# A sparse graph layer: one place column instead of sixteen, and three of 41 gathers taken from DRAM by indirect DMAs

## The chip, the cores and the metric

The kernel runs on one core of a Trainium2 chip. The metric is device time in microseconds (us), the median of several executions; lower is better. The core has five engines that run side by side and are tied together by semaphores: TensorE (PE, with its weight loads as PEld), VectorE (DVE), ScalarE (ACT), GpSimd (POOL) and SyncE (SP). In this kernel SP issues nearly all DMAs, each in its order, and waits in front of one for what that DMA needs. POOL issues DMAs of its own on a second queue.

## The reference

32 independent graphs (batches) of N = 512 nodes, D = 128 features, and a weighted adjacency of which about one entry in 16 is not zero (and the diagonal). Layer 0 is a normalized graph convolution with a residual and a layernorm. Layer 1 forms a message for every ordered pair of nodes and sums the messages with the adjacency as weight:

```python
m_j = einsum('bnd,do->bno', x, W1[:D])
m_i = einsum('bnd,do->bno', x, W1[D:])
pre = m_j[:, None, :, :] + m_i[:, :, None, :] + b1      # one vector per pair (i, j)
msg = gelu(layernorm(pre, g1, be1))
agg = einsum('bijo,bij->bio', msg, adjacency)
upd = layernorm(concatenate([x, agg]) @ W2 + b2, g2, be2)
x   = layernorm(x + upd)
```

Dense, this would be 512 x 512 messages a batch. The kernel computes only those whose adjacency is not zero.

## The kernel before, in words

**The tiling.** The nodes of a batch are cut into C = 4 chunks of P = 128. A source node j sits on a partition; chunk q holds 128 sources. For each source and each target chunk c, the nonzero targets are kept as a list. The first SLOTS = 8 entries of a list are its slots t = 0 to 7. Slot 8 (`EXTRA`) is the ninth entry of the lists inside a chunk's own diagonal block. What is left over in the lists of one (q, c) block is packed into 256 shared places, which are slots 9 and 10. A *group* is one slot t of one source chunk q, for the four target chunks: 4 x 128 messages. There are 8 x 4 + 1 + 2 x 4 = 41 groups in a batch (`order`), numbered n = 0 to 40 here; group 18 is (t 4, q 2), group 22 is (5, 2) and group 26 is (6, 2).

**One group's work.** `pairs` (L720 to L725) makes `u`, a PSUM bank of 4 x 128 x 128: for each target chunk three bf16 products of a one-hot matrix `s` with the three bf16 parts `c3` of the target's vector c = m_i + b1 (L724, a gather by product), and a fourth product with the standard deviations (L725). In the shared slots a float32 product adds the source's vector (L720). `sums` (L734, DVE) adds the source's vector a and writes `u_sb`. `messages` (L763, ACT) applies gelu with the pair's own scale, four instructions per group. `weights` (L749, POOL) multiplies the transposed one-hots `mt` with the adjacency into `sw`. `aggregate` (L772, PE) sums `m` x `sw` into one PSUM bank `agg` for the whole batch.

**The pipeline over groups.** In round n of the main loop the program writes down `pairs` of group n, `aggregate` of n-3, `sums` and `weights` of n-1 and `messages` of n-2. `u` has 3 buffers, `u_sb` 3, `m` 3, `sw` 4, so an engine that falls back by about two groups stops PE. On ACT, POOL and DVE the order of instructions is the order in which the program writes them (`manual_schedule`). On PE and SP a list scheduler orders them.

**The side work.** The preparation of the next batch and of the later slots of this one is cut into steps by `yield` and spread over the rounds by the table `plan` (phase, steps, first and last round). `layer0`, `lists` (the eight largest of each list with their indices, L399 and L400, and `idx_d`, which is sent through DRAM), `parts` (`ac`, the vectors a and c; POOL adds a bias at L622; then `c3` by three ACT casts L627 with a POOL subtraction L626 between them), `factors`, `more` (16 further entries of each list, L455 to L458) and `shared` follow each other and overlap. `parts` of the next batch lies in rounds 22 to 30 of the present one, `shared` in rounds 8 to 27.

**`shared` in detail.** `a_t` holds for each block the transposed adjacency (128 columns) and 3 x 16 more: the place numbers of the 16 further entries, their node numbers and their variances; `WIDE` = 176. POOL fills the place columns with two operations on 128x256 (L502, L505). A float32 product with the one-hot `sj` sends the rows of `a_t` to their places (L537, 32 products of 128x176 per batch, each in two passes in the trace), ACT copies the banks to `sent` (L533). DVE then picks from each sent row the entry whose place equals the row's own place (L553, four operations, and L561, two reductions into `picked`). ACT and PE turn `picked` into `idx_ds` (L566, L574, L582), which goes through DRAM to `raw` and comes back as one-hot `s` of slots 8 to 10. POOL waits for `picked` at L578.

## Time and profile before

| | |
|---|---|
| median of 3 runs | 4012.79 us (4010.46 to 4013.59) |
| the profiled execution's own time | 4011.93 us |
| its span (first to last instruction on the core) | 4010.2 us |
| PE busy in the span | 3759.7 us, 94% |
| DVE, ACT, POOL busy | 81%, 69%, 56% |
| granted TensorE clock, mean | 0.985 |
| time of one batch in the steady part (from one `agg` start after a wait for ACT to the same one six batches later, 1079.73 to 1819.44 us) | 123.3 us |

A batch is a fixed succession of stretches that repeats 32 times, so the profile is best read on one batch (here the one from 2028 to 2152 us) and multiplied. A row of the groups gives line, engine, operation, output <- inputs, shape, count, then busy time, mean duration of one, and the idle time just before it with what ended it. Matmul durations overlap each other, so the price of a matmul is taken from the distance of starts in the timeline.

### The profile page before, as it was taken

What the parts mean: (1) busy time and instruction counts of PE and PEld (TensorE: products, weight loads), DVE (VectorE), ACT (ScalarE), POOL (GpSimd) and SP (SyncE); (2) the same over time, 40 slices, a digit from 0 to 9 for tenths busy, and PEclk for the clock granted to TensorE, in tenths of its full rate; (3) what the DMA queues carried; (4) which work ended last, traced back from release to release, by engine and by line L of the source; (5) the groups of instructions that cost most, each with busy time, mean ns of one, the idle gap of its engine ahead of it and who ended that gap; (6) DMA issues with size and microseconds to landing.
All of it is one profiled execution on the core that took longest, in us unless ns stands there. A gap on an engine that the chain in (4) does not pass through costs nothing. (4 is left out here: it accounts for less than half of the span.)

```text
span 4010.2 us, 108407 instructions
## 1 busy us (share of the span) xinstructions
PE 3759.7 (94%) x39744; PEld 3502.1 (87%) x39744; DVE 3262.1 (81%) x10645; ACT 2785.8 (69%) x8321; POOL 2226.4 (56%) x2526
## 2 busy tenths in 40 slices
PE   5999999999999999999999999999999999999997
PEld 5988889888899888998888988889988889888887
DVE  6888888888887888888888878888888888788882
ACT  4777677676676766777766777667777667776664
POOL 4555565555654555655556556566556565565654
PEclk7999999999999999999999999999999999999998
DMA  3444444444544544444444444444444444444442
GB/s 85 106 109 106 115 100 106 109 104 105 115 100 106 106 104 111 106 108 107 108 105 107 104 110 104 104 113 105 108 108 106 107 103 107 111 104 104 100 106 56
DMA packets 902107, 419.99 MB, mean 105 GB/s; under 512 B 724304, under 2 KB 882192, under 8 KB 901568
## 3 DMA queue, kind: packets, MB, share of 16 engines
q1 hardware_dynamic: 901344, 412.52, 44.3%
q8 instruction: 317, 5.19, 0.5%
q14 instruction: 222, 1.82, 0.1%
q0 software_dynamic: 224, 0.46, 0.1%
HBM read 227.15 MB, written 13.76 MB: 60 GB/s over the span
## 5 line engine op out<-in xcount | busy, mean ns | idle before, releaser
L749 POOL TENSOR_TENSOR sw<-mt,a_t 128x512 f32<-128x512 bf16 x1056 | 1216.5, 1164 | 918.4 <-PE agg L772 767.5
L772 PE MATMUL agg<-sw,m 128*128 128x128 f32 x10496 | 1494.0, 285 | 109.5 <-ACT m L763 64.3
L724 PE MATMUL u<-c,s 128*128 128x128 bf16 x15744 | 1411.5, 220 | 58.1 <-DVE u_sb L734 54.5
L763 ACT ACTIVATE m<-u_sb,r 128x128 f32<-128x128 f32 x4096 | 1293.3, 394 | 196.3 <-DVE counts L484 105.9
L772 PEld LDWEIGHTS agg<-sw,m 128*128 128x128 f32 x10496 | 1301.9, 193 | 131.9 <-POOL ve_l L199 67.7
L724 PEld LDWEIGHTS <-s 128*128 128x128 bf16 x15744 | 1191.9, 99 | 136.4 <-issue 64.4
L725 PE MATMUL u<-be,sd_rows 128*128 128x128 bf16 x5248 | 1148.6, 220 | 21.4 <-DMA sd_rows<-sd_ds 15.5
L734 DVE TENSOR_TENSOR u_sb<-u,ac 128x512 f32<-128x512 f32 x1056 | 713.4, 676 | 199.1 <-PE u L725 176.8
L725 PEld LDWEIGHTS <-sd_rows 128*128 128x128 bf16 x5248 | 514.8, 98 | 31.5 <-issue 20.8
L763 ACT ACTIVATE m<-u,r_s 128x128 f32<-128x128 f32 x1024 | 288.9, 363 | 251.9 <-PE agg L772 247.9
L687 DVE TENSOR_SCALAR s<-raw,node_p 128x2052 bf16<-128x2052 bf16 (+1 forms) x352 | 421.5, 1197 | 20.4 <-DMA raw<-idx_ds 11.8
L720 PE MATMUL u<-ac,sj 128*128 128x128 f32 x2048 | 437.2, 295 | 0.0
L749 POOL TENSOR_TENSOR sw<-mt,sent 128x512 f32<-128x512 bf16 x256 | 296.5, 1163 | 226.6 <-PE agg L772 188.7
L533 ACT COPY sent<-pl 128x352 f32<-128x352 f32 x512 | 229.1, 447 | 258.3 <-PE pl L537 221.4
L537 PEld LDWEIGHTS pl<-a_t,sj 128*128 128x128 f32 x2048 | 316.1, 190 | 60.1 <-issue 37.1
L457 DVE MAX8 a_t<-key 128x8 f32<-128x128 f32 x1024 | 301.2, 295 | 34.5
L537 PE MATMUL pl<-a_t,sj 128*128 128x176 f32 x2048 | 327.4, 313 | 0.6 <-POOL a_t L505 0.6
L522 DVE TENSOR_SCALAR sj<-pj,node_p 128x512 f32<-128x512 f32 x256 | 187.6, 745 | 156.4 <-PE pj L526 156.4
L720 PEld LDWEIGHTS u<-ac,sj 128*128 128x128 f32 x2048 | 309.8, 191 | 0.4
L458 DVE FIND_INDEX8 idx_m<-a_t,key 128x8 uint32<-128x128 f32 x1024 | 291.4, 285 | 0.0
L361 DVE SCALAR_TENSOR_TENSOR key<-pv,a_sum,c_sum 128x512 f32<-128x512 f32 x128 | 95.6, 748 | 108.3 <-PE pv L365 108.3
L400 DVE FIND_INDEX8 idx<-top,key 128x8 uint32<-128x128 f32 x512 | 145.7, 285 | 0.0
(178 smaller groups left out, 4766.5 us busy)
## 6 DMA issues: line engine op xcount, KB each, us to landing
raw<-idx_d SPq DMA_DIRECT2D x256, 513.0 KB
raw<-idx_ds SPq DMA_DIRECT2D x64, 513.0 KB
a_nat<-in_adj_dram SPq DMA_DIRECT2D x32, 1024.0 KB
sd_rows<-sd_d SPq DMA_DIRECT2D x768, 12.0 KB
xs<-in_x_dram SPq DMA_DIRECT2D x32, 256.0 KB
out_dram<-o_sb SPq DMA_DIRECT2D x32, 256.0 KB
mt<-s SPq DMA_TRANSPOSE x352
raw<-idx_ds SPq DMA_DIRECT2D x32, 129.0 KB
```

The lines of the kernel that those rows point to most:

```text
L457: nc.vector.max(found, k)
L458: nc.vector.max_index(idx[:, n, h : h + 8], found, k)
L533: nc.scalar.copy(sent[:, n - 1], pt[:, : SHARED * WIDE].rearrange("p (k w) -> p k w", w=WIDE))
L537: nc.tensor.matmul(pt[:, k * WIDE : (k + 1) * WIDE], sj[:, n, k * P : (k + 1) * P], at[:, n, :], start=True, stop=True,)
L687: nc.vector.tensor_scalar(s.rearrange("p (k e) -> p k e", k=3), raw, node_p, None, ALU.is_equal)
L720: nc.tensor.matmul(pu[:, c, :], place, state[b]["ac"][:, q, 0, :], start=first, stop=False)
L724: nc.tensor.matmul(pu[:, c, :], here, c3[:, k, c, :], start=(first and k == 0), stop=False)
L725: nc.tensor.matmul(pu[:, c, :], dev[:, q, c, :], be9, start=False, stop=(c == C - 1))
L734: nc.vector.tensor_tensor(u, pu, a if t == EXTRA else bcast(a[:, q, :], C), ALU.add)
L749: nc.gpsimd.tensor_tensor(sw, mt[:, 0] if t == EXTRA else mt[:, :, q, :], a, ALU.mult)
L763: nc.scalar.activation(m[:, c, :], u[:, c, :], AF.Gelu, scale=r[:, k : k + 1])
L772: nc.tensor.matmul(st["agg"][:, c, :], m[:, c, :], sw[:, c, :], start=(begin and c == 0), stop=(end and c == C - 1),)
```

## The change

Two edits stand in one diff. First, the sixteen place columns in `a_t` become one column, which holds the place that entry 0 of the list has or would have (`first` + `sharing`). `WIDE` becomes 161. POOL writes it with one operation on 128x16. At the receiving side `rank` = own place - first place tells which of the sixteen entries is meant, and DVE compares `nth` (now counted from 0) with it: two operations on 16 elements, two comparisons of 256, two multiplications of 512 and the two reductions as before. `shared` has 46 steps instead of 45.

Second, for the groups 18, 22 and 26 the three gather products per target chunk (12 per group) are left out. Instead `parts` writes c (512 x 128 float32, 256 KB) to DRAM (`c_d`) on the SP queue, between POOL's bias addition and its first subtraction, which overwrites the same tile; `parts` has 8 steps instead of 7. `lists` computes row numbers `row_no` with three small DVE operations. In the rounds 5, 4, 3 and 2 before such a group, POOL issues one indirect DMA each, which fetches 128 rows of 512 bytes by `row_no` into `c_i`. DVE adds the source's vector to `c_i` in the group's own round, and `sums` adds `c_i` instead of a broadcast vector.

```diff
-WIDE = 128 + 3 * MORE
+WIDE = 128 + 2 * MORE + 1
@@ constants
-        nth, pattern=[[0, C * C], [1, MORE]], base=1, channel_multiplier=0, allow_small_or_imprecise_dtypes=True
-    nc.gpsimd.tensor_scalar(nth[:, own, :], nth[:, own, :], 1.0, None, ALU.subtract)
+        nth, pattern=[[0, C * C], [1, MORE]], base=0, channel_multiplier=0, allow_small_or_imprecise_dtypes=True
+    chunk_0 = const.tile([P, C], I32, name="chunk_0")
+    nc.gpsimd.iota(chunk_0, pattern=[[P, C]], base=0, channel_multiplier=0)
@@ lists, after the last max_index
+        row_no = small.tile([P, len(by_rows), C], I32, tag="row_no", name=f"row_no_{b}", bufs=1)
+        for k, (t, q) in enumerate(by_rows):
+            nc.vector.tensor_tensor(row_no[:, k, :], idx[:, q * C : (q + 1) * C, t], chunk_0, ALU.add)
+        st["row_no"] = row_no
@@ shared
-        place, node_i, var = (at[:, :, P + k * MORE : P + (k + 1) * MORE] for k in range(3))
+        node_i, var = (at[:, :, P + k * MORE : P + (k + 1) * MORE] for k in range(2))
...
-        nc.gpsimd.tensor_tensor(
-            place, nth, first.unsqueeze(2).to_broadcast([P, C * C, MORE]), ALU.add
-        )
-        nc.gpsimd.tensor_tensor(place, place, over, ALU.mult)
+        nc.gpsimd.tensor_tensor(at[:, :, WIDE - 1], first, sharing[:, :, 0], ALU.add)
...
+        rank = small.tile([P, SHARED, C * C], F32, tag="rank", name=f"rank_{b}", bufs=1)
+        for k in range(SHARED):
+            nc.vector.tensor_scalar(
+                rank[:, k, :], sent[:, :, k, WIDE - 1], place_k[:, k : k + 1], -1.0, ALU.subtract, ALU.mult
+            )
+        for k in range(SHARED):
+            nc.vector.tensor_tensor(
+                chosen[:, 1, k], nth, rank[:, k, :].unsqueeze(2).to_broadcast([P, C * C, MORE]), ALU.is_equal
+            )
+        yield
         for h in range(2):
-            for k in range(SHARED):
-                nc.vector.scalar_tensor_tensor(
-                    chosen[:, h, k],
-                    sent[:, :, k, P : P + MORE],
-                    place_k[:, k : k + 1],
-                    sent[:, :, k, P + (1 + h) * MORE : P + (2 + h) * MORE],
-                    ALU.is_equal,
-                    ALU.mult,
-                )
+            nc.vector.tensor_tensor(
+                chosen[:, h],
+                chosen[:, 1],
+                sent[:, :, :, P + h * MORE : P + (h + 1) * MORE].rearrange("p n k l -> p k n l"),
+                ALU.mult,
+            )
             nc.vector.tensor_reduce(picked[:, h, :], chosen[:, h].rearrange("p k n l -> p (k n) l"), AX.X, ALU.add)
@@ parts
         nc.gpsimd.tensor_tensor(rest, rest, bcast(b1g, C), ALU.add)
+        yield
+        c_d = dram.tile([N, D], F32, tag="c_d", name=f"c_d_{b}")
+        nc.sync.dma_start(c_d.rearrange("(c p) d -> p c d", p=P), rest)
+        st["c_d"] = c_d
         for k in range(3):
             if k:
                 yield
                 nc.gpsimd.tensor_sub(rest, rest, c3[:, k - 1])
             nc.scalar.copy(c3[:, k], rest)
@@ pairs
-            for k in range(3):
-                nc.tensor.matmul(pu[:, c, :], here, c3[:, k, c, :], start=(first and k == 0), stop=False)
-            nc.tensor.matmul(pu[:, c, :], dev[:, q, c, :], be9, start=False, stop=(c == C - 1))
+            if (t, q) not in by_rows:
+                for k in range(3):
+                    nc.tensor.matmul(pu[:, c, :], here, c3[:, k, c, :], start=(first and k == 0), stop=False)
+                first = False
+            nc.tensor.matmul(pu[:, c, :], dev[:, q, c, :], be9, start=first, stop=(c == C - 1))
@@ sums
+        if (t, q) in by_rows:
+            nc.vector.tensor_tensor(u, pu, made_c.pop((b, t, q)), ALU.add)
+            return u
@@ new
+    def rows_of_c(b, t, q, c):
+        if c == 0:
+            made_c[b, t, q] = pair.tile([P, C, D], F32, tag="c_i", name=f"c_i_{b}_{t}_{q}", bufs=2)
+        k = by_rows.index((t, q))
+        nc.gpsimd.indirect_dma_start(
+            made_c[b, t, q][:, c, :],
+            None,
+            state[b]["c_d"][:],
+            bass.IndirectOffsetOnAxis(ap=state[b]["row_no"][:, k, c : c + 1], axis=0),
+        )
@@ plan
+    by_rows = [order[n] for n in (18, 22, 26)]
-        (parts, 7, -19, -10),
+        (parts, 8, -19, -10),
-        (shared, 45, 8, 28),
+        (shared, 46, 8, 28),
@@ main loop, before pairs
+                for c, ahead in enumerate((5, 4, 3, 2)):
+                    if n + ahead < n_groups and order[n + ahead] in by_rows:
+                        rows_of_c(b, *order[n + ahead], c)
+                if (t, q) in by_rows:
+                    c_i = made_c[b, t, q]
+                    nc.vector.tensor_tensor(c_i, c_i, bcast(state[b]["ac"][:, q, 0, :], C), ALU.add)
```

More of the change, by code (lines that the diff above doesn't have):

```diff
@@ L119, in sparse_path @@
     )
-    nth = const.tile([P, C * C, MORE], F32, name="nth")
-    nc.gpsimd.iota(
-        nth, pattern=[[0, C * C], [1, MORE]], base=1, channel_multiplier=0, allow_small_or_imprecise_dtypes=True
-    )
     sharing = const.tile([P, C * C, MORE], F32, name="sharing")
@@ L129, in sparse_path @@
     nc.gpsimd.memset(sharing[:, own, 0:1], 0.0)
-    nc.gpsimd.tensor_scalar(nth[:, own, :], nth[:, own, :], 1.0, None, ALU.subtract)
+    nth = const.tile([P, C * C, MORE], F32, name="nth")
+    nc.gpsimd.iota(
+        nth, pattern=[[0, C * C], [1, MORE]], base=0, channel_multiplier=0, allow_small_or_imprecise_dtypes=True
+    )
     node_p = const.tile([P, 1], F32, name="node_p")
     nc.vector.tensor_scalar(node_p, place_p, 1.0, None, ALU.subtract)
+    chunk_0 = const.tile([P, C], I32, name="chunk_0")
+    nc.gpsimd.iota(chunk_0, pattern=[[P, C]], base=0, channel_multiplier=0)
     power = const.tile([P, 1], F32, name="power")
@@ L455, in more @@
                 nc.vector.match_replace(k, found, k, -1.0)
-                found = at[:, n, WIDE - MORE + h : WIDE - MORE + h + 8]
+                found = at[:, n, P + MORE + h : P + MORE + h + 8]
                 nc.vector.max(found, k)
@@ L735, in sums @@
         return u
+    def rows_of_c(b, t, q, c):
[7 more added lines that the diff above has]
+            bass.IndirectOffsetOnAxis(ap=state[b]["row_no"][:, k, c : c + 1], axis=0),
+        )
     def weights(b, t, q):
@@ L793, in sparse_path @@
     nc.vector.memset(most, 0.0)
-    made_r, made_s, made_m, made_d = {}, {}, {}, {}
+    made_r, made_s, made_m, made_d, made_c = {}, {}, {}, {}, {}
     todo = []
     n_groups = len(order)
+    by_rows = [order[n] for n in (18, 22, 26)]
     plan = [
```

1 line of the change is left out of this document (removed).

## The prediction

> **What bounds the kernel now.** The page first: which engine has no room.
>
> ```profile
> span 4010.2 us, 108407 instructions
> PE 3759.7 (94%) x39744; PEld 3502.1 (87%) x39744; DVE 3262.1 (81%) x10645; ACT 2785.8 (69%) x8321; POOL 2226.4 (56%) x2526
> ```
>
> PE is the bound on average, but 6% of 4010 us is idle, and an average hides where. So next the busy time by stretches of one batch. The columns are span, then busy PE, PEld, DVE, ACT, POOL, then clock, DMA share, GB/s.
>
> ```profile
> 2052.40:2066.40 14.00, 11.88 (x129) 11.62 (x127) 13.93 (x48) 7.03 (x23) 9.84 (x18) 0.92 0.33 79
> 2066.40:2080.00 13.60, 13.56 (x120) 10.53 (x119) 8.59 (x15) 9.74 (x28) 8.51 (x8) 0.96 0.44 106
> 2080.00:2104.00 24.00, 24.00 (x218) 21.86 (x217) 15.01 (x26) 16.70 (x51) 5.82 (x5) 1.00 0.49 131
> 2104.00:2124.00 20.00, 19.33 (x230) 18.05 (x229) 18.60 (x65) 17.31 (x49) 15.14 (x17) 1.00 0.50 83
> ```
>
> Three regimes: DVE fills 2052 to 2066; from 2066 to 2104 (rounds 13 to 23) PE is never idle and DVE and POOL have room; from 2104 to 2124 (rounds 24 to 32) PE, DVE and ACT are all nearly full and POOL is three quarters full. Who holds PE when it waits (us in total, times, longest):
>
> ```profile
> PE agg L772 <- ACT m L763: 64.3, 31, 2.1
> PE u L724 <- DVE u_sb L734: 54.5, 40, 2.2
> PE agg L772 <- POOL sw L749: 27.7, 22, 1.5
> ```
>
> Last the timeline of the full stretch (start, duration, engine, what, idle before it):
>
> ```profile
> 2113.10 1.16 POOL L749 TENSOR_TENSOR sw<-mt,a_t 128x512 f32<-128x512 bf16 x1
> 2114.22 0.42 POOL L378 TENSOR_TENSOR sd_rest_s<-sd_rest_s,sd_p_s 36x128 f32<-36x128 f32 x1
> 2115.73 1.26 POOL L622 TENSOR_TENSOR ac<-ac,b1g 128x512 f32<-128x512 f32 x1
> 2118.07 1.15 POOL L626 TENSOR_TENSOR ac<-ac,c 128x512 f32<-128x512 f32 x1
> ...
> 2114.68 0.30 ACT L379 CAST sd_p_s<-sd_rest_s 36x128 bf16<-36x128 f32 x1
> 2117.02 0.62 ACT L627 CAST c<-ac 128x512 bf16<-128x512 f32 x1 [0.87 <-POOL ac L622]
> 2119.26 0.62 ACT L627 CAST c<-ac 128x512 bf16<-128x512 f32 x1 [0.44 <-POOL ac L626]
> 2119.78 1.27 ACT L763 ACTIVATE m<-u_sb,r 128x128 f32<-128x128 f32 x4
> ...
> 2120.32 1.27 PE L772 MATMUL agg<-sw,m 128*128 128x128 f32 x8
> ```
>
> This is a chain without slack: POOL's subtraction lets ACT cast, the cast stands ahead of group 28's gelu, and `agg` of 28 runs while that gelu ends (1.27 instead of 1.11 us).
>
> **Gains, per batch, in the stretch where PE alone limits.**
> (a) Group 18: three gather products and the fourth start at 2057.21, the next four at 2057.43, so 0.22 us for four and 0.167 for three. Twelve fall away: 0.67 us.
> (b) Narrower sent rows: 24 passes of 176 columns run from 2089.71 to 2093.29, 0.149 us each. With 161 columns 0.0127 less each, by width; 64 passes: 0.8 us. (No gain would follow if ACT's copies held the banks; ACT waits 1.3 us for these products at a time, so they don't.)
> (c) POOL before `sw` of group 11: L502 and L505 (0.62 and 0.73) become one of about 0.2, as other 128x4 operations take, so `sw` is 1.1 us earlier. PE waits for POOL exactly there, 27.7 us / 32 = 0.87 a batch. It ends at most there, and sooner if gelu of 11 holds it: I take 0.6.
> Sum 2.07 us, times 32 = 66 us.
>
> **The indirect DMAs.** Twelve a batch, on POOL, in rounds 13 to 24. The trace has none. The nearest row is POOL's plain issue at the start, `b_row`: 0.53 to 0.58 us for one, 32 packets each (224 for 7); four times the packets would make 2.1 us. Between these ends I take 1.2. From 2066 to 2104 POOL works 14.3 of 37.6 us, so 12 x 1.2 = 14.4 fits beside; a price of zero gains nothing, 2.1 (25 us) just fills it. Behind each DMA stands the `sw` of one group; at 1.2 us POOL still reaches `sw` of 12 at 2069.3, `agg` of 12 needs it at 2069.7. Those loads of the start landed 5.0 to 5.5 us after issue: for group 18 the fourth goes out near 2074.0 and lands by 2079.5, DVE adds at 2081.1; the other two groups have more room. What waits behind a late one is DVE's `u_sb` of 17, needed by PE only about ten us later. So zero, as long as an issue stays under about 2.2 us.
> [...]
>
> **Losses, per batch, in rounds 22 to 32.** Here groups 22 and 26 spare PE another 1.34 us, but PE is not alone.
> DVE: the additions to `c_i` are like L362 (two SBUF inputs, 128x512, 0.69); that of 18 and of 22 fall into DVE's waits for PE (1.87 us in front of `u_sb` at 2099.54), that of 26 does not: 0.69. Picking: two small operations 0.3 (128x16, 0.16 to 0.18 each), two comparisons 0.43 to 0.80 each as L553 took alone and beside POOL, two multiplications 0.69, against four of L553 (2.48 in this batch): +0.9. `row_no` 0.4. DVE, continuously busy there, is 2 us longer; `picked` is 0.6 late, so `idx_rs`, the table loads behind it and `m` of 23 are 0.5 late.
> POOL and ACT: the changed order puts the bias addition (1.22) ahead of the second `sd_rest_s`; ACT's last `sd_p_s` cast, and `m` of 26 behind it, move 2 us, of which 0.87 returns because the `c` cast no longer waits for the addition. The first subtraction now also waits until `c_d` has been read. SP issues that DMA at about 2116.2, behind the tail of the 513 KB `raw` transfer, which flows until 2118 (246 and 215 GB/s in those two us); 256 KB at that rate is 1.1 us, and the 48 KB write of `sd_d` kept SP waiting 2.6 us after its issue. Landing some 3.9 us after issue: 2120.1. The subtraction ends at 2121.2, the cast at 2121.8, `m` of 28 starts there instead of 2119.78; `agg` of 28, the `idx` products and group 32 follow, less the half us by which PE had run ahead: the stretch ends 1.55 us later than before. Bounds: landing before POOL arrives (2118.75) makes +0.7; 5.5 us makes +3.1; were all three engines slack, -1.34. I take 1.55, from the rows of the same stretch. SP behind `c_d` (`sd_ds`, then the transposes of slot 8) is not held: `sd_ds` needs the delayed cast anyway.
> 31 x 1.55 = 48 us (the last batch has no `parts` behind it).
> [...]
>
> **Sum.** 4011.9 - 66 + 48 = 3994 on the profiled execution's time, 0.9 under the median: 3995.
>
> **Rivals.**
> *R1, the full stretch absorbs it.* For it: PE lost only 0.67 us there before. Then only the gains count: 4012 - 66 = 3946, with groups 22 and 26 paid too 3903. Against: `m` of 28 has no slack.
> *R2, the write of c is slow: slower.* One mechanism, POOL's subtraction behind `c_d`. Every us of landing is a us of `m` of 28. The gain is used up when the loss reaches 66 / 31 = 2.14 us, a landing 4.5 us after issue. At 5.5 us: 31 x 3.1 - 66 = +30, 4042. For it: 5.0 us for a quarter of the bytes on the other queue, and a queue that is not empty. Against: `sd_d`.
> *R3, POOL becomes the bound.* An issue of 3 us makes 36 + 14.3 = 50 us of work in 38, with four `sw` buffers some 8 us lost a batch: 4270. It decides from about 2.2 us.
> *R4, the change does nothing:* PE's removed products were covered. Excluded from 2066 to 2104 by 24.00 of 24.00 busy.
>
> **How the numbers follow.** Forecast (3970 to 4020) 0.40, R1 0.15, R2 0.22, R3 0.13, near 4012 by cancelling terms 0.10. A measurement here can tell about 0.2% (8 us) from no change. Faster: 0.28 of the forecast, R1, a little of R2: 0.46. Same 0.16. Slower 0.38. The range leaves out R1's lower end and most of R3: 3930 to 4080.
>
> **What would show it.** 1152 matmuls fewer at L724 (14592 instead of 15744); the sent product at about 0.136 us a pass; the wait of `agg` for POOL's `sw` gone in front of group 11; the indirect DMA's own row on POOL (1.2 us; over 2.2 proves R3); POOL's subtraction waiting for a DMA of `c_d`, about 1.3 us a batch; new PE waits for ACT `m` in groups 26 and 28. Wrong if `agg` waits for POOL in rounds 13 to 23, or DVE for `c_i`.

## The result, and the profile after

The changed kernel takes 4061.41 us (median of four executions, 4057.43 to 4064.48) against 4013.19 us before: a ratio of 1.012, 95% interval 1.0107 to 1.0132. It is 48 us slower, where 18 us less were forecast. The page of the changed kernel:

```profile
span 4060.5 us, 107124 instructions
PE 3710.9 (91%) x38592; PEld 3443.8 (85%) x38592; DVE 3467.5 (85%) x10901; ACT 2763.5 (68%) x8321; POOL 2568.3 (63%) x2878
```

PE has 49 us less work than before and more idle time; DVE has 205 us more and POOL 342 us more. The groups that the change added or altered (busy us in the program, mean ns of one):

```profile
L743 PE MATMUL u<-c,s 128*128 128x128 bf16 x14592 | 1320.8, 221 | 54.1 <-DVE u_sb L757 50.1 <-DVE s L705 4.0
L765 POOL DMA_INDIRECT c_i<-c_d,row_no x384 | 416.9, 1086 | 62.4 <-issue 43.1 <-PE agg L807 1.9 <-PE pl L542 1.4
L567 DVE TENSOR_TENSOR chosen<-chosen,sent 128x512 f32<-128x512 f32 x64 | 92.0, 1438 | 1.1
L906 DVE TENSOR_TENSOR c_i<-c_i,ac 128x512 f32<-128x512 f32 x96 | 76.6, 798 | 14.1 <-DMA c_i<-c_d,row_no 14.1
L408 DVE TENSOR_TENSOR row_no<-idx,chunk 128x4 int32<-128x4 uint32 x96 | 55.8, 632 | 0.0
L573 DVE TENSOR_REDUCE picked<-chosen 128x32 f32<-128x512 f32 x64 | 43.9, 686 | 2.2
L556 DVE TENSOR_SCALAR rank<-sent,place_k 128x16 f32<-128x16 f32 x64 | 35.2, 590 | 0.0
L562 DVE TENSOR_TENSOR chosen<-nth,rank 128x256 f32<-128x256 f32 x64 | 23.9, 411 | 0.0
```

The 1152 products are gone as forecast, and an indirect DMA holds POOL for 1.09 us. But the picking (L556, L562, L567, L573) is 195 us, 6.1 us a batch; before it was 79.7 + 43.9 = 123.6 us, 3.9 a batch. And three row numbers of 128x4 take 1.74 us a batch. Who waits for whom in the changed kernel (us in total, times, longest):

```profile
PE agg L807 <- ACT m L798: 93.1, 92, 2.0
ACT idx_s L578 <- DVE picked L573: 84.2, 32, 3.9
PE pidx_s L586 <- ACT idx_s L582: 57.6, 32, 4.6
POOL ac L642 <- DMA c_d<-ac: 50.0, 30, 2.9
PE agg L807 <- POOL sw L784: 48.5, 48, 5.3
```

Of the kernel before, the row for ACT's wait for `picked`:

```profile
ACT idx_s L566 <- DVE picked L561: 7.2, 32, 0.4
```

ACT now stands 2.6 us a batch in front of the cast of `picked`, and the messages are queued behind that cast; before it stood 0.2. Of the 48.5 us for which `agg` waits for `sw`, 38.2 lie in S4 (the cuts S1 to S5 are explained next), 2 to 3 us behind POOL's wait for the write of c; at the place of the old wait, in front of group 11, 4.3 us are left.

To see where a batch gains and loses I cut it at the first starts of five products on PE and take means over 24 batches (us; worked out from the timelines of PE). S1 runs from `pu` to the next `pt_x`; S2 from there to `pac` (PE is the limit); S3 from `pac` to `psd_s` (the picked list); S4 from there to `pidx` (the full stretch); S5 from there to the next `pu`. "Last" is the last distance from one `pu` to the next. "+ seven steps" is "no overwrite" with one edit more; the two rows under it are each "+ seven steps" with one edit more. Ratios are to the kernel before, timed beside on the same chip; between rows I go by them, because the kernel before itself moved between 4009 and 4015 us.

| kernel | median us | ratio | S1 | S2 | S3 | S4 | S5 | batch | last |
|---|---|---|---|---|---|---|---|---|---|
| before | 4013 | 1 | 32.28 | 38.93 | 5.84 | 11.55 | 34.12 | 122.72 | 115.7 |
| the change | 4061 | 1.012 | 32.18 | 35.96 | 7.62 | 14.39 | 34.00 | 124.14 | 119.2 |
| one column alone | 4007 | 0.9985 | 32.20 | 37.60 | 6.26 | 12.68 | 33.96 | 122.69 | 108.7 |
| rows alone | 4091 | 1.0198 | 32.34 | 38.59 | 5.84 | 13.95 | 34.33 | 125.04 | 117.1 |
| group 18 only | 4028 | 1.0039 | 32.21 | 36.37 | 6.25 | 14.59 | 33.78 | 123.19 | 119.5 |
| no overwrite | 4051 | 1.0098 | 32.11 | 35.80 | 7.62 | 12.76 | 35.18 | 123.47 | 119.6 |
| + seven steps | 4079 | 1.0178 | 32.13 | 35.96 | 7.62 | 12.67 | 36.33 | 124.71 | 117.4 |
| + one row-number operation | 4076 | 1.0155 | 32.04 | 36.07 | 7.62 | 12.68 | 36.20 | 124.61 | 117.8 |
| + row numbers on POOL | 4027 | 1.0032 | 32.35 | 35.64 | 7.61 | 12.67 | 34.72 | 122.99 | 115.3 |
| early fetch | 4034 | 1.0066 | 32.12 | 35.71 | 7.04 | 14.18 | 34.05 | 123.10 | 121.1 |
| the change, halves | 4029 | 1.004 | 32.26 | 35.80 | 6.93 | 13.64 | 34.24 | 122.88 | 122.6 |
| one column, halves | 3937 | 0.9807 | 32.10 | 37.22 | 5.84 | 11.56 | 33.77 | 120.48 | 110.8 |
| the same, group 18 by rows, all repairs | 3947 | 0.9833 | 32.30 | 36.54 | 5.84 | 11.45 | 34.27 | 120.39 | 121.4 |
| the change, all repairs | 4011 | 0.9996 | 32.30 | 36.19 | 6.94 | 12.66 | 34.33 | 122.43 | 120.0 |

The change gains 3.07 us a batch in S1 and S2 and loses 4.50 in S3 to S5, 1.78 of it in front of the products of `picked` (S3) and 2.84 in S4. Thirty batches at 1.42 are 43 us; the last batch adds 3.5 and the time up to the first `pu` 4.5, together the 50 us by which the span grew.

S2 also holds what the granted clock does. In some batches the trace has one stretch of 3.41 us at half clock at the start of S2 (in the kernel before once 6.83 us), and there S2 is up to 1.0 us longer: in one column alone 36.90 us without it, 37.90 in the slowest batches. (In the kernel before, where PE also waits for `sw` in S2, it lies between 38.22 and 40.89.) One column alone has it in 24 of 30 batches, the same column with the picking in halves in 11, the kernel before in 13; the mean clock in S2 is 0.965, 0.984 and 0.983. In the batches at full clock alone, S2 is 38.95 us before, 36.90 for one column in either form, 36.22 with group 18 by rows and 35.59 in the change. So in the mean S2 is 0.70 us a batch longer than at full clock in one column alone, 0.32 with the picking in halves and 0.37 in the change: the 0.38 us between the two forms of one column are the clock's, and so may differences of that size be between other kernels with the same products in S2. Why one kernel has the stretch more often than another is not shown.

### The profile page after: what moved, and what is told of

Read it like the earlier page. It is cut to its first block, busy times and chain, and to the rows that moved or that the text cites. A ratio compares the mean times of both kernels' runs of the same rounds, so it can differ in the third digit from the quotient of the medians.

```text
span 4060.5 us, 107124 instructions
## 1 busy us (share of the span) xinstructions
PE 3710.9 (91%) x38592; PEld 3443.8 (85%) x38592; DVE 3467.5 (85%) x10901; ACT 2763.5 (68%) x8321; POOL 2568.3 (63%) x2878
## 3 DMA queue, kind: packets, MB, share of 16 engines
q0 software_dynamic: 12512, 25.65, 2.4%
## 5 line engine op out<-in xcount | busy, mean ns | idle before, releaser
L807 PE MATMUL agg<-sw,m 128*128 128x128 f32 x10496 | 1517.7, 287 | 164.2 <-ACT m L798 93.1
L784 POOL TENSOR_TENSOR sw<-mt,a_t 128x512 f32<-128x512 bf16 x1056 | 1184.9, 1127 | 461.9 <-PE agg L807 311.9
L743 PE MATMUL u<-c,s 128*128 128x128 bf16 x14592 | 1320.8, 221 | 54.1 <-DVE u_sb L757 50.1
L743 PEld LDWEIGHTS <-s 128*128 128x128 bf16 x14592 | 1110.8, 99 | 125.1 <-issue 62.2
L745 PE MATMUL u<-be,sd_rows 128*128 128x128 bf16 x5248 | 1098.7, 220 | 5.6 <-DMA sd_rows<-sd_d 4.1
L757 DVE TENSOR_TENSOR u_sb<-u,ac 128x512 f32<-128x512 f32 x960 | 650.2, 677 | 91.7 <-PE u L745 85.1
L765 POOL DMA_INDIRECT c_i<-c_d,row_no x384 | 416.9, 1086 | 62.4 <-issue 43.1
L738 PE MATMUL u<-ac,sj 128*128 128x128 f32 x2048 | 439.5, 296 | 10.6 <-DVE u_sb L757 10.6
L538 ACT COPY sent<-pl 128x322 f32<-128x322 f32 x512 | 216.0, 422 | 227.8 <-PE pl L542 197.2
L542 PEld LDWEIGHTS pl<-a_t,sj 128*128 128x128 f32 x2048 | 295.1, 190 | 59.3 <-issue 40.4
L542 PE MATMUL pl<-a_t,sj 128*128 128x161 f32 x2048 | 303.2, 300 | 0.0
```

What stands on the lines that cost most here:

```text
L542: nc.tensor.matmul(pt[:, k * WIDE : (k + 1) * WIDE], sj[:, n, k * P : (k + 1) * P], at[:, n, :], start=True, stop=True,)
L738: nc.tensor.matmul(pu[:, c, :], place, state[b]["ac"][:, q, 0, :], start=first, stop=False)
L743: nc.tensor.matmul(pu[:, c, :], here, c3[:, k, c, :], start=(first and k == 0), stop=False)
L745: nc.tensor.matmul(pu[:, c, :], dev[:, q, c, :], be9, start=first, stop=(c == C - 1))
L757: nc.vector.tensor_tensor(u, pu, a if t == EXTRA else bcast(a[:, q, :], C), ALU.add)
L765: nc.gpsimd.indirect_dma_start(made_c[b, t, q][:, c, :], None, state[b]["c_d"][:], bass.IndirectOffsetOnAxis(ap=state[b]["row_no"][:, k, c ...
```

## The experiments

Two explanations to begin with. **A**: POOL's work beside the picking stretches it, `picked` is late, and ACT and PE with it. **B**: POOL's subtraction waits for the write of c (rival R2). First the two halves of the change by themselves, a smaller change, and B's wait removed.

**One column alone.**

```diff
-    by_rows = [order[n] for n in (18, 22, 26)]
+    by_rows = []      # row_no, c_d and its step removed too
```

> The one-column edit alone: no group by rows, no write of c, no row numbers. Two explanations of the 48 us are on the table. A: POOL's work, the indirect DMAs above all, stretches the picking operations on DVE beside it (multiplication 2.20 us beside POOL, 0.67 without), so that `picked` is late and PE waits 1.8 us a batch before its products. B: POOL's subtraction waits 1.6 us a batch for the write of c, and group 28 with it. Under A the picking is nearly cheap once the indirect DMAs are gone: the gains of 1.4 us a batch (45 us) stay, less about 0.6 us a batch for two operations more: 3985 us. If the picking is dear by its own operations, whatever POOL does (A'), it takes back 1.3 us a batch: about 4010. B says nothing on the picking, and expects the 45 us whole: 3968.

4006.72 us, ratio 0.9985 (0.9976 to 0.9994). The expectation's A' (the picking is dear by its own operations, whatever POOL does) gives this number: in S2 the gain is 1.33 us (1.41 with S1; 2.05 in the batches at full clock), and S3 and S4 take back 1.55, with no indirect DMA in the kernel. But its reason is only half right, for POOL's products stretch the new operations. DVE and then POOL in the timeline of this kernel (start, duration):

```profile
1613.60 1.08 DVE L552 TENSOR_SCALAR rank<-sent,place_k 128x16 f32<-128x16 f32 x2
1614.60 0.75 DVE L558 TENSOR_TENSOR chosen<-nth,rank 128x256 f32<-128x256 f32 x2
1615.38 1.51 DVE L563 TENSOR_TENSOR chosen<-chosen,sent 128x512 f32<-128x512 f32 x1
...
1613.38 1.13 POOL L776 TENSOR_TENSOR sw<-mt,a_t 128x512 f32<-128x512 bf16 x1 [3.77 <-PE agg L799]
1615.22 1.13 POOL L776 TENSOR_TENSOR sw<-mt,a_t 128x512 f32<-128x512 bf16 x1 [0.71 <-PE agg L799]
```

The second multiplication of a batch needs 0.67 us, with POOL idle; this one ends 0.54 us after POOL's `sw` ended. The two `rank` operations end 0.2 us after the other `sw`. In the whole change:

```profile
1625.16 2.20 DVE L567 TENSOR_TENSOR chosen<-chosen,sent 128x512 f32<-128x512 f32 x1
...
1624.42 1.22 POOL L765 DMA_INDIRECT c_i<-c_d,row_no  x1
1625.66 1.14 POOL L784 TENSOR_TENSOR sw<-mt,a_t 128x512 f32<-128x512 bf16 x1
...
1628.11 0.32 ACT L578 CAST idx_s<-picked 128x16 bf16<-128x16 f32 x2 [2.58 <-DVE picked L573]
...
1628.58 0.39 PE L586 MATMUL pidx_s<-ident_h,idx_s 128*9 128x128 bf16 x4 [1.70 <-ACT idx_s L582]
```

The indirect DMA stands ahead of `sw`, so the whole of `sw` falls into the multiplication: 2.20 us. That is 0.39 more than the product and an undisturbed multiplication together (1.14 + 0.67); the multiplication stands beside the DMA for its first 0.48 us.

**Rows alone.** The old sixteen columns and the old picking, all three groups by rows. The fetched rows had no room of their own and lie in two tiles of the layernorms, f0 and f1, so this is not quite the half of the change.

```diff
-            made_c[b, t, q] = pair.tile([P, C, D], F32, tag="c_i", ..., bufs=2)
+            tag = "f0" if (t, q) == by_rows[1] else "f1"
+            made_c[b, t, q] = node.tile([P, C, D], F32, tag=tag, ...)
```

> The by-rows edit alone: sixteen place columns and the old picking, three groups by rows; since the wider tiles leave no room, the fetched rows lie in two tiles that the layernorms of the end of a batch use otherwise (f0, f1), so the first DMA for group 18 may wait for the last layernorm. Group 18 (and 22, lying near the same stretch) give back 0.67 us each at most, 21 to 43 us. B expects the wait of the subtraction as in the whole change, 1.6 us a batch, 50 us: 4020 to 4040. A expects that the old picking is stretched by the indirect DMAs too (L553's 0.43 us alone, 0.80 beside POOL's product), by up to 1.5 us a batch, beside the 50: 4050 to 4070.

4090.93 us, 1.0198 (1.0184 to 1.0212), above even A's range, though the old picking is not stretched (ACT waits 8.1 us in all for `picked`) and S3 is as before. S4 alone loses 2.40 us, B's place; S2 gains 0.34 of 1.34. So neither explanation gives this number; the two parts do not add up either (-6 and +78 against +48). The trace shows where it goes. PE's wait for `sw` stays, since the old place operations stay; a new wait, which no other kernel has, stands in front of the sent rows' products; and in S4 PE waits 1.9 us a batch for ACT's `m`:

```profile
PE agg L804 <- ACT m L795: 125.1, 94, 3.0
PE agg L804 <- POOL sw L781: 26.6, 21, 1.5
PE pl L545 <- DVE key L364: 20.6, 31, 0.7
```

What makes DVE's `key` and the messages late was not followed, nor how much the two tiles have to do with it.

**Group 18 only.**

```diff
-    by_rows = [order[n] for n in (18, 22, 26)]
+    by_rows = [order[n] for n in (18,)]
```

> The whole change, but only group 18 is read by rows: four indirect DMAs a batch instead of twelve, one row-number operation instead of three, one addition instead of three, and the last indirect DMA is issued some seven rounds before the picking. Groups 22 and 26 get their products back, 0.67 us of PE each, of which 22's lies where PE alone limits (21 us). The write of c and the wait for it stay. A expects that the 1.8 us in front of the products of `picked` go, 56 us: 4061 - 56 + 21 = 4026. B expects that nothing of the loss goes: 4061 + 21 = 4082, or 4061 if group 22 gave nothing.

4028.06 us, 1.0039 (1.0025 to 1.0052): A's number. S3 falls from 7.62 to 6.25, the value of one column alone. S4 stays at 14.59 with the write of c: B's loss is there as well.

**The subtraction into another tile.**

```diff
+                if k == 1:
+                    less = node.tile([P, C, D], F32, tag="t2", name=f"less_{b}")
-                nc.gpsimd.tensor_sub(rest, rest, c3[:, k - 1])
+                nc.gpsimd.tensor_sub(less, rest, c3[:, k - 1])
+                rest = less
```

> The whole change, but POOL's first subtraction writes to another tile (one that layer 0 has left by then), so that it need not wait until the write of c to DRAM has read its source. Everything else stays. B expects the 1.6 us a batch of the subtraction's wait back, 31 x 1.6 = 50 us: 4011. A expects little, at most a few us, because the lateness comes from the picking before it: 4050 to 4060.

4051.3 us, 1.0098 (1.0083 to 1.0114): some 10 us back, not 50 (the two intervals overlap a little, so the 10 are rough). The wait is gone, and S4 is 1.63 us shorter, just the 1.6 that it cost. But S5 is 1.18 longer: something else ended last there, and B's wait had hidden it.

Next, that something (**C**: the order of POOL's addition), the picking (**D**: DVE has no idle time from round 24 on, so each us of its work is a us of the batch), and A's DMAs.

**Seven steps,** on top of the kernel without the overwrite.

```diff
-        yield
         c_d = dram.tile([N, D], F32, tag="c_d", name=f"c_d_{b}")
-        (parts, 8, -19, -10),
+        (parts, 7, -19, -10),
```

> The kernel of the run without the overwrite (4051), and besides, the write of c is put down in the same step as the bias addition, so that `parts` has seven steps as before and POOL's addition (1.26 us) again follows the subtractions of `sd_rest_s` where it stands before the second of them now. C: this order makes ACT wait 1.2 us a batch for `sd_rest_s` (54.7 us in all against 17.0) and everything behind it in ACT's order: 31 x 1.2 = 37 us back, 4014. If ACT has that much room by then, nothing: 4051.

4079.33 us, 1.0178 (1.0161 to 1.0195): slower by some 30 us. C falls. ACT's wait for `sd_rest_s` did fall from 54.9 to 17.0 us, but S4, where it stands, became only 0.09 us shorter. What grew is the row numbers: 90.0 us, 2.8 a batch, and PE's wait for `u_sb` behind them, from 25.1 us to

```profile
PE u L740 <- DVE u_sb L759: 49.6, 60, 1.0
```

**The picking in halves,** on one column alone: blocks 0 to 7 are picked while the other rows are still being sent.

```diff
+            if n == 15:
+                ranks(0, 8)          # rank and comparison of blocks 0 to 7
             if n % 2:
                 yield
-        yield from pause(3)
+        yield
+        picks(0, 0, 8)               # multiplication and reduction
+        yield
+        picks(1, 0, 8)
+        yield
...
-        chosen = big.tile([P, 2, SHARED, C * C, MORE], F32, tag="mask", ...)
+        chosen = big.tile([P, 2, SHARED, C * C, MORE], F32, tag="a_nat", ...)
```

> The one-column edit alone (4007), with the picking cut in two: blocks 0 to 7 are picked two to three steps earlier, beside products that DVE waits for anyway (1.0 and 1.7 us at a time), and only blocks 8 to 15 after the last copy of the sent rows. `chosen` takes a tile that is free by then. DVE theory D: from round 24 on DVE has no idle time, and each us of its work there is a us of the batch; in one column alone the picking is 1.6 us longer than before and a batch loses 1.5 us there. Half the picking moved out takes some 1.5 us from that stretch: 4007 - 47 = 3960. If the loss came from something else in the edit, 4000 to 4010.

4025.2 us, 1.0038 (1.0024 to 1.0052): slower than one column alone and outside both expectations, by the tile I had chosen. ACT's wait for `picked` fell from 60.3 to 10.7 us and S3 is 5.84 again, but

```profile
DVE s L715 <- DMA raw<-idx_ds: 101.8, 31, 5.1
```

The tile is the one that the adjacency of a later batch is loaded to. The last picking operation ends at 1863.29 us, and that load goes out at once, late in the batch (with other tiles, below, 12 us after `pt_x`). SP in the timeline:

```profile
1863.32 0.39 SPq L238 DMA_DIRECT2D a_nat<-in_adj_dram  x1
1866.32 3.00 SPq L717 DMA_TRANSPOSE mt<-s  x1
1869.37 0.49 SPq L388 DMA_DIRECT2D idx_ds<-idx_rs  x1
```

The list goes out behind 1 MB and a transpose, counted from `psd_s` 4.5 us later than in one column alone, and DVE waits 3.2 us for it to come back.

**Early fetch:** the whole change, with the DMAs of group 26 three rounds earlier; the rows of group 22 lie in f0 for it.

```diff
                 for c, ahead in enumerate((5, 4, 3, 2)):
-                    if n + ahead < n_groups and order[n + ahead] in by_rows:
-                        rows_of_c(b, *order[n + ahead], c)
+                    for m in (n + ahead, n + ahead + 3):
+                        if m < n_groups and order[m] in by_rows and (m == n + ahead) == (order[m] != by_rows[2]):
+                            rows_of_c(b, *order[m], c)
```

> The whole change (4061), but the four indirect DMAs for group 26 go out three rounds earlier (rounds 18 to 21 instead of 21 to 24), so that none stands beside the picking any more; the rows of group 22 lie in another tile for that. Nothing else moves. A: of the 2.20 us of the first multiplication 0.7 goes (1.51 in one column alone, beside POOL's product only), and `picked` comes that much earlier, or more with the product itself no longer pushed into it: 0.7 to 1.4 us a batch, 4018 to 4040. If the indirect DMAs are not what delays the picking: 4061.

4034.06 us, 1.0066 (1.0049 to 1.0083): in A's range, 22 us back by the ratios. The multiplication takes 0.68 us in the mean; the comparisons now meet `sw` instead (0.87 instead of 0.41), so the picking is 5.5 us, and ACT's wait for `picked` falls to 63.6 us.

**A combination** (halves, other tile for the subtraction, seven steps, groups 18 and 22, one row-number operation), first with `chosen` in the adjacency's tile, then in f0 and f1, together with the halves alone in f0 and f1.

```diff
-    by_rows = [order[n] for n in (18, 22, 26)]      # the combinations only
+    by_rows = [order[n] for n in (18, 22)]
...
-        chosen = big.tile([P, 2, SHARED, C * C, MORE], F32, tag="a_nat", ...)
+        chosen = [node.tile([P, SHARED, C * C, MORE], F32, tag=f"f{h}", ...) for h in range(2)]
```

> What the explanations together would keep: one column, the picking in halves, the subtraction into another tile, seven steps of `parts`, only the groups 18 and 22 by rows, and their row numbers by one operation instead of two. If C and D hold, the gains that the traces show (1.4 us a batch of the column, 0.67 us each of the two groups) remain: 4013 - 45 - 43 = 3925, with some 20 us more for what is left of the losses: 3925 to 3945. If the losses have another cause, 4010 to 4030.

> The one-column edit with the picking in halves again, but `chosen` lies in the two tiles f0 and f1 and not in the one that the adjacency of a later batch is loaded into. In the run before, that load (1 MB) went out only when the picking was done, just ahead of the write of the picked list, and DVE waited 3.2 us a batch for that list to come back. D: with that gone, DVE's added work of the picking (1.6 us a batch) lies where DVE waits, and the gain of 1.4 us a batch comes through: 4007 - 45 = 3962. If DVE then waits for the list anyway, which came back with 0.1 us to spare before, 3990 to 4007.

> The combination (one column, halves, another tile for the subtraction, seven steps, groups 18 and 22, one row-number operation) with `chosen` in f0 and f1. D: PE is the bound from round 13 to round 23, DVE in nearly all the rest of a batch. PE's gain of 1.4 + 1.34 us a batch counts only if DVE's work does not grow in the rest; what grows there is the row numbers (0.8 us) and what the indirect DMAs and POOL stretch: 4009 - 85 + 25 to 60 = 3950 to 3985. If the shortened first part only makes DVE wait less there and more work is left for the full part: 4000 to 4030.

The first combination took 4058.96 us (1.0126, 1.0109 to 1.0143), outside both expectations and held up like the halves before: DVE waits 104.2 us for `raw` of `idx_ds`. **One column with the picking in halves and the right tiles takes 3937.43 us: 0.9807 (0.9793 to 0.982), 78 us faster than the kernel before.** S3 and S4 are back at 5.84 and 11.56 and the gain of S2 stays. (Against one column alone it is 69 us; some 12 of these, 0.38 a batch in S2, are the granted clock.) ACT's wait for `picked`, of one column alone and then of this kernel:

```profile
ACT idx_s L574 <- DVE picked L569: 60.3, 32, 2.0
ACT idx_s L592 <- DVE picked L557: 10.7, 32, 1.4
```

The second combination took 4030.55 us (1.0044, 1.0031 to 1.0058), not D's 3950 to 3985 but the end of the other range: S5 is 36.49. Its row numbers, one operation of eight elements per partition, took 3.50 us each (DVE first, then POOL):

```profile
1631.95 3.50 DVE L408 TENSOR_TENSOR row_no<-idx,chunk 128x8 int32<-128x8 uint32 x1
...
1631.01 1.18 POOL L663 TENSOR_TENSOR less<-less,c 128x512 f32<-128x512 f32 x1
1632.12 3.30 POOL L806 TENSOR_TENSOR sw<-mt,a_t 128x512 f32<-128x512 bf16 x3
```

It ends when POOL's back-to-back run ends (1635.4), not before. That is not always so. In the whole change the same addition, there in three operations, ends between POOL's instructions (DVE, then POOL):

```profile
1523.60 1.64 DVE L408 TENSOR_TENSOR row_no<-idx,chunk 128x4 int32<-128x4 uint32 x3
...
1522.98 1.15 POOL L642 TENSOR_TENSOR ac<-ac,c 128x512 f32<-128x512 f32 x1
1524.09 3.29 POOL L784 TENSOR_TENSOR sw<-mt,a_t 128x512 f32<-128x512 bf16 x3
```

The row is three records: two end at 1524.15 and 1524.22, as the subtraction does (1524.13), the third at 1525.23, as the first of the three products does (1525.21).

**One row-number operation** in the kernel with seven steps, and **a useless operation** in the kernel before:

```diff
-        for k, (t, q) in enumerate(by_rows):
-            nc.vector.tensor_tensor(row_no[:, k, :], idx[:, q * C : (q + 1) * C, t], chunk_0, ALU.add)
+        nc.vector.tensor_tensor(
+            row_no, idx[:, q * C : (q + 1) * C, t0 : t0 + n_k], chunk_0.unsqueeze(2).to_broadcast([P, C, n_k]), ALU.add
+        )
```

> The kernel with seven steps (4079), with the row numbers of the three groups made by one DVE operation on 128x12 instead of three on 128x4. In that kernel the three took 2.73 us a batch, because they stand beside POOL's work; in the whole change 1.65. D: where DVE has no idle time, every us of it is a us of the batch; one operation should take 0.6 to 0.9 us, so 1.8 to 2.1 us a batch are saved: 4079 - 31 x 1.95 = 4019. If the order of ACT and POOL is what made that kernel slower (C reversed), 4070 to 4079.

```diff
+        extra = small.tile([P, 32], F32, tag="extra", name=f"extra_{b}", bufs=1)
+        nc.vector.tensor_reduce(extra, key[:, 0, :].rearrange("p (n l) -> p n l", l=16), AX.X, ALU.add)
```

> The kernel before, with one useless reduction on DVE (128x512, 0.69 us, one input in SBUF) at the end of `lists`, at about round 32; its result is read by nobody. It prices one us of DVE in the full part by itself. D: 31 x 0.69 = 21 us, 4032. If DVE has room there after all (the profile before shows 81% in the mean): 4011, no change.

4075.64 us (1.0155, 1.0141 to 1.0169) and 4016.83 us (1.0005, 0.9996 to 1.0014). The first is no test of D after all: the single operation took 2.64 us in the mean instead of the 0.6 to 0.9 expected (it too ends with a run of products of POOL; the undisturbed one of the 32 took 0.15). The second makes D fall as I had put it: 0.67 us more of DVE's work at the end of `lists` costs nothing that can be measured. DVE makes it up at its next wait; of the kernel before and then of this one:

```profile
DVE r L425 <- ACT sd L423: 35.5, 32, 1.6
```

```profile
DVE r L427 <- ACT sd L425: 19.0, 32, 1.0
```

What counted here was not how much DVE works but what is late behind it.

So two causes remained to be put to the test (**E**: the row numbers; **F**: the picking), and whether reading by rows is worth anything without them.

**Row numbers on POOL,** in the kernel with seven steps.

```diff
+        nc.gpsimd.tensor_tensor(        # at the start of shared, round 8
+            row_no, st["idx"][:, q0 * C : (q0 + 1) * C, t0 : t0 + n_k],
+            chunk_0.unsqueeze(2).to_broadcast([P, C, n_k]), ALU.add,
+        )
```

> The kernel with seven steps and the other tile (4079), but the row numbers are made by POOL, in one operation at the start of `shared` in round 8 of the batch that uses them, so that DVE does not make them in `lists` at all. E: in the run with one row-number operation DVE stood 2.64 us in that single operation, as long as POOL worked back to back beside it, and PE's products of slots 9 and 10 waited for DVE's `u_sb` behind it; the subtraction's wait for the write of c had hidden that. From `pidx` to the end of the batch that kernel needs 36.3 us, the kernel before 34.1: 31 x 2.2 = 68 us back, 4011. If the row numbers are not what holds this part: 4075.

4027.12 us, 1.0032 (1.0019 to 1.0044): 52 us less than with seven steps (58 by the ratios), most of E's number. S5 falls from 36.33 to 34.72, 50 us in all; 0.32 a batch more comes from S2, where the products are the same and the mean clock went from 0.979 to 0.994. PE's wait for `u_sb` in front of the products with `sj` is gone.

**The whole change with the picking in halves** (the edits shown for the halves, in f0 and f1).

> The whole change (4061) with the picking in halves as its only edit (`chosen` in f0 and f1). F: the late `picked` costs the whole change 1.78 us a batch in front of its products and another 1.1 us after them, because ACT, which waited 2.6 us for it, then gives the messages too late: up to 31 x 2.9 = 90 us back, 3971. Since the wait for the write of c and the row numbers stand behind it, part of it will be taken up again: 3971 to 4010. If the picking is not the main cost: 4040 to 4061.

4029.34 us, 1.004 (1.0026 to 1.0053): 32 us back, less than F's range. ACT still waits 62.3 us for `picked`: with twelve indirect DMAs on POOL the multiplications of a half take 0.84 us in the mean, in one column alone 0.44.

**All repairs** (halves in f0 and f1, other tile for the subtraction, seven steps, row numbers on POOL), with group 18 and with all three groups by rows.

```diff
-    by_rows = [order[n] for n in (18, 22, 26)]      # kept in the second
+    by_rows = [order[n] for n in (18,)]
```

> The best kernel so far (one column with the picking in halves, 3937) and besides only group 18 by rows, with everything that the runs named put out of the way: the subtraction into another tile, seven steps, row numbers on POOL. Group 18 spares PE 0.67 us a batch where PE alone limits: 3937 - 21 = 3916, if four indirect DMAs and one addition cost nothing beside. If by-rows costs more than it spares even so: 3940 to 3960.

> All three groups by rows and one column, with all repairs: halves, other tile, seven steps, row numbers on POOL. PE is spared 2.0 us a batch beyond the best kernel (3937), of which group 26's 0.67 lies where PE does not limit alone: 3937 - 43 = 3894 if nothing else is in the way. If twelve indirect DMAs hold DVE and POOL as the traces show (comparisons and multiplications beside them stretched, 13 us of POOL), 3940 to 3980.

3946.96 us (0.9833, 0.9819 to 0.9846) and 4011.17 us (0.9996, 0.9987 to 1.0005). Neither reaches its hopeful number, and the second lies above its whole range (to 3980). With three groups, S3 and S4 are 6.94 and 12.66: PE waits 1.0 us a batch in front of the products of `picked` again. With group 18 alone the batches in the middle are 0.09 us shorter than without it (S2 -0.68, as priced; S5 +0.50), and the last batch is 10.6 us longer. S5 gives it back in a wait of PE that the best kernel has only once, 0.69 us a batch here:

```profile
PE psd L436 <- ACT sd L427: 23.7, 30, 2.4
```

With seven steps, where it was 2.4 us, moving the row numbers to POOL raised it to 20.7; the list scheduler has put the first `psd` product about 2 us earlier in PE's order, ahead of `sd`. So it goes with that repair rather than with the reading by rows. No run puts `psd` back.

In the last batch POOL's final reduction stands in its queue (timeline of POOL, then DVE):

```profile
3832.86 0.99 POOL L791 DMA_INDIRECT c_i<-c_d,row_no  x1 [0.16 <-issue]
3841.71 0.43 POOL L1174 PARTITION_ALL_REDUCE peak<-most  x1 [7.86 <-PE pl L577]
3849.12 1.11 POOL L810 TENSOR_TENSOR sw<-mt,a_t 128x512 f32<-128x512 bf16 x1 [6.98 <-issue]
3850.41 1.19 POOL L791 DMA_INDIRECT c_i<-c_d,row_no  x1 [0.18 <-issue]
...
3853.24 5.46 DVE L932 TENSOR_TENSOR c_i<-c_i,ac 128x512 f32<-128x512 f32 x1 [10.71 <-DMA c_i<-c_d,row_no]
```

The trace shows 0.43 us of the reduction and POOL idle on both sides of it, so of the 15.3 us between the third DMA and the next product it is not known how many the reduction works.

**Not in the last batch.**

```diff
-                if (t, q) in by_rows:
+                if b < B - 1 and (t, q) in by_rows:      # and so in the three other places
```

> The repaired kernel with group 18 by rows (3947), except that the last batch takes group 18 by products like any other. In that kernel the batches in the middle took 120.37 us against 120.50 of the best kernel, and all of its 10 us more lay in the last batch (121.4 against 110.8 us): there POOL's reduction at the end of the program stands between the third and the fourth indirect DMA, and DVE waits 10.7 us for the rows. G: without that, 3947 - 10.6 = 3936, equal to the best kernel (3937) within 0.2%. If the rows cost it elsewhere: 3945 to 3947.

3936.1 us, 0.9818 (0.9805 to 0.9832), as G said. By the ratios alone it is not told from the kernel with the rows in all batches (0.9833), since their intervals overlap; the trace tells: the last batch takes 111.5 instead of 121.4 us, the others 120.40 and 120.39. One group by rows, with these repairs, is even in the other 31 batches.

## Why the prediction was wrong, step by step

**Gains: right, (c) in part by luck.** (a) 0.67 us for group 18: from the first `pv` product to the last, one column alone takes 14.68 us and with group 18 by rows 14.01. (b) 0.8 us for the narrower rows: that part falls from 15.28 to 14.68 and the next, up to `pac`, from 8.75 to 8.57, 0.78 together; a pass takes 0.137 us, forecast 0.136. (c) PE's wait for `sw` fell from 27.7 to 3.3 us in one column alone, 0.76 a batch, forecast 0.6. That this came out near 0.6 is partly the clock's doing: from `pt_x` to the first `pv` the mean falls from 14.90 to 14.34, but in the batches at full clock from 14.92 to 13.64, by 1.28. With group 22's 0.67 the forecast was 2.74 us a batch for S1 and S2; measured were 3.07 (3.36 in S2 at full clock). R4 is out.

**The indirect DMA: right.** 1.09 us instead of 1.2, with 0.16 us of idle time ahead of most; R3 is out. The upper bound of 2.1 us rested on four times the packets of `b_row`; a DMA of 128 rows made 32, as many as one of `b_row` (12512 - 224 over 384 DMAs). DVE waits for `c_i` only in the last batch (14.1 us in two waits).

**The write of c: right in size, wrong in weight.** Forecast 1.3 us of waiting for POOL, measured 1.6 (50.0 us). The forecast led it through the cast to `m` of 28; PE's new waits for `m` in S4 are there (60, together 32.0 us), but a second path was not named: `sw` stands behind the subtraction in POOL's order, and PE waits 38.2 us for it in S4. But taking it away gave back only some 10 us. R2 is a loss that is there, not the one that decided.

**The step that failed is "DVE ... is 2 us longer; `picked` is 0.6 late, so `idx_rs`, the table loads behind it and `m` of 23 are 0.5 late".** Two things in it. Its terms were too small: picking +0.9, measured +2.2 us a batch (+1.5 without indirect DMAs in the kernel); `row_no` 0.4, measured 1.74, and in one operation up to 3.5. (The prices named for the picking do not even give 0.9: 0.3 + two at 0.43 to 0.80 + 2 x 0.69 - 2.48 is 0.1 to 0.8.) The comparisons, priced for POOL beside them, came cheaper, 0.37 us each. The others were priced by single rows of undisturbed operations, and many stand beside POOL: the two `rank` operations took 1.10 us a batch instead of 0.3, the two multiplications 2.88 instead of 1.38. And the lateness was taken through the table loads only; no term of the 1.55 us stands for it. On ACT the cast of `picked` stands in the middle of the messages: ACT waits 2.6 us there, PE 1.8 us (S3), and then ACT does the held-up work in the full stretch: in one column alone 10.8 us of work in S4 instead of 9.6, with the same 1.8 us of waiting for POOL, and S4 1.13 us longer. The halves test this: with `picked` in time, ACT works 9.75 us there and S4 is 11.56 again.

**DVE beside POOL.** The additions to `c_i` were priced as DVE's other 128x512 additions, 0.69 us, with nothing for POOL beside them; they took 0.80 us in the mean, a small error. The runs show the larger one where I did not look: a multiplication of 0.67 us with POOL idle took 1.51 us beside `sw` and 2.20 with an indirect DMA ahead of `sw`, and a row-number operation took 3.50 us beside a subtraction and three products. `rank`, which reads one tile and one number per partition, took 0.22 us undisturbed and 0.94 beside a product.

**The order of `sd_rest_s`** (a loss of 1.2 us on ACT, of which 0.87 returns): the wait came, 54.7 instead of 17.0 us, but undoing it made S4 only 0.09 us shorter.

**Not foreseen at all:** the last batch, 10.6 us for one group by rows; that the row numbers hide behind the write of c, so that one removed wait uncovers the next; and the granted clock, whose share of S2 is 0.70 us a batch in one column alone and 0.32 in the same kernel with the picking in halves. The forecast added its losses along one chain, to `m` of 28; they lie on several chains side by side, and one of them, through `picked`, alone cost one column its whole gain.

What stays open: what makes `key` and the messages late in rows alone, whether group 18 would pay without the wait at `psd`, the 4.5 us ahead of the first batch, and why the stretch at half clock comes more often in some kernels. Whether the indirect DMA by itself slows DVE was not separated from the product it pushes: the two comparisons beside it in the whole change (0.75 us) were not slowed, while the multiplication after them has 0.39 us that the product does not explain.

## What to carry to other kernels

Price a small operation at its place, not by its shape: look at what the other engines do in that microsecond, and on DVE at how long POOL is busy without a break (here a row-number operation of 0.15 us undisturbed took 2.64 in the mean). Follow a late result through every in-order queue that it passes: in one column alone a 0.2 us cast that waits in the middle of ACT's messages cost 1.55 us a batch (S3 and S4), as much as the picking had grown (1.5). Before two kernels are compared, compare their granted clock stretch by stretch. And when one part of a change gains and another loses, run each alone: here one part, with its picking moved to where DVE waits anyway, is worth 78 us, and the other so far nothing.

## What the hardware showed that I had not expected

- In two places a DVE operation lasted to the end of a run of POOL instructions without a gap, or beyond it. Eight elements per partition took 3.50 us beside one subtraction and three products; in the last batch the addition to `c_i`, 0.63 us alone, took 5.46 us beside a run of six products (6.53 us) and ended 0.54 us after it. It is no rule: in the whole change 57 of 96 row-number operations ended where one POOL instruction ended and the next followed at once, and none took more than 1.14 us. What decides is not shown.
- Indirect DMAs of 128 rows of 512 bytes held POOL 0.98 to 1.47 us each, and they are in POOL's order: the final reduction shows 0.43 us in the trace, but POOL was idle 7.86 us before it and 6.98 after, and the DMA behind it was 15 us late.
- Where a tile lay decided when a transfer went out: the same code was some 90 us slower (1.0038 against 0.9807) with a scratch tile that a 1 MB load waits for, because that load then went ahead of a short list.
- Batches with one stretch of 3.41 us at half clock at the start of S2, where PE is the limit, have an S2 up to 1.0 us longer (37.90 instead of 36.90 us in one column alone); 24 of 30 batches have the stretch in one column alone and 11 in the same kernel with the picking in halves.
